# Centroid logits and the feed-forward's product as one weight matrix of 576 columns, in two banks

## The chip, the cores and the metric

The kernel runs on one core of one Trainium2 chip. The metric is the device time of one execution in microseconds (us), taken as the median of several executions. Engines are named as in the profile: PE is TensorE's matmuls and PEld its weight loads, DVE is VectorE, ACT is ScalarE, POOL is GpSimd, and SP is SyncE, which here only issues transfers.

## The reference

One transformer block on `x` of 8 x 256 tokens with 512 features, all in fp32: an attention layer, then a clustered feed-forward layer, each behind a layer norm and with its input added to its output.

```python
def attn(h):                       # 32 heads, 8 key/value heads, D = 128
    q, k, v = split(h @ w_qkv)
    s = q @ k.T * D**-0.5 - slope[head] * sqrt(max(i - j, 0))    # causal
    return (softmax(s) @ v) @ w_o

def ffn(h):                        # h: 2048 x 512
    dots = softmax(h @ centroids.T / 0.1)          # 2048 x 64
    hits = dots > 0.01
    query_sel = any(hits, axis=1)                  # per token
    row_sel = any(hits, axis=0)[assignments]       # per output column
    dense = h @ weight.T + bias                    # 2048 x 512
    return where(query_sel[:, None] & row_sel[None, :], dense, 0)

x = x + attn(layernorm(x))
x = x + ffn(layernorm(x))
```

The feed-forward layer thus has two products with the same left operand, the normalised tokens: 64 columns of logits and 512 columns of output. A column of the output counts only if any token of the whole batch hits its cluster, so that choice can be made only at the very end.

## The kernel before

The 2048 tokens are 16 tiles of 128, and four tiles make a pair of sequences (`p` = 0 to 3). For each pair the kernel goes through the 8 key/value heads, and for each head through the two sequences: 64 units `u`, 16 slots per pair, and two more units to drain. The order of the work on each engine is the order in which the program text issues it (the schedule is manual); buffers come from pools that rotate, and a buffer's next owner waits until its last reader is done. The projections and the output product are done by a seven-product scheme on half blocks (`strassen`, L136, and `project_out`, L454), whose extra sums are made by GpSimd and VectorE.

In unit `u` the kernel computes the scores of unit `u`, subtracts the maximum and takes the exponential of unit `u`-1, and multiplies the weights of unit `u`-2 with the values (`attend`, L429, tiles `av` and `oT`) and with `w_o` (`project_out`, whose banks are `ps_oa`, `ps_ob` and `ps_oc`, and which adds into the residual `x2`). The maxima and sums over keys are made by `over_keys` (L384, tile `r`), transposed by TensorE into `tp_r` (L397), written to a row in memory and read back broadcast to all partitions as `bc` (L406 and L415, both on SP's queue). GpSimd (L422) and VectorE (L425) then subtract the maximum.

The feed-forward layer of a finished tile `t_ffn` is put between these steps as a function `f` of four parts. Tiles 0 to 3 are done in slots 3 to 6 of pair 1, tiles 4 to 7 in the same slots of pair 2, and tiles 8 to 11 in units 62 to 65. Part 0 transposes the normalised tile into `xnT`. Part 1 makes the logits (`ffn_logits`: four matmuls of 64 columns into a bank `lg`, then the negated maximum `cmax` on VectorE, L523 and L524), their exponential on ScalarE (L537), and the dense product (`ffn_dense`: four matmuls of 512 columns into a bank `ps_f`). Part 2 adds the bias (L552), and part 3 finds the hits and finishes the tile. Tiles 12 to 15 (`last` and the next three) are done behind the loop, logits and dense products apart. In the last unit, 65, the next layer norm's statistics (L259 and L260) stand on VectorE directly behind the logits' maximum of tile 11, and the output product adds its parts straight from the banks (L481, L488, L494).

PSUM has eight banks of 512 fp32 columns: three are shared as `acc` (`av`, `ps_f`, `ps_ob`, `ps_oc` and others), two as `sc` (the scores and `lg`), one is `tp` (transposes), and two hold the long sums. The weights of the dense product are loaded into the buffer of the value weights (`wv`) three times: at the end of slot 1 of pairs 1 and 2, and at the end of unit 58. The centroids are loaded once, at the start.

Of the kernel before, what the change touches and what calls it, by code (L numbers as in the profile page):

```python
# [26 lines left out]
NC_H = H // P  # L27
# [6 lines left out]
TEMPERATURE = 0.1  # L34
# [19 lines left out]
def block_kernel(  # L54
# [12 lines left out]
    nc = tc.nc  # L67
# [5 lines left out]
    const = ctx.enter_context(tc.tile_pool(name="const", bufs=1))  # L73
    wpool = ctx.enter_context(tc.tile_pool(name="w", bufs=1))
# [106 lines left out]
    wv, wk, wq, wo = {}, {}, {}, {}  # L181
    HH = H // 2
# [9 lines left out]
        wv[p, half] = [w[:, 2 * k : 2 * k + 2, ts(m, HH)] for m in range(2) for k in range(2)]  # L192

    def load_w_ffn():
        w = wpool.tile([P, NC_H, H], F32, tag="wv", name="w_ffn")
        nc.sync.dma_start(w, w_ffn_t.rearrange("(c p) n -> p c n", p=P))
        return w

    def load_wk(p, j):
# [46 lines left out]
    nc.gpsimd.dma_start(dist_sb, dist)  # L246
    hits_any = const.tile([P, NCL], F32, name="hits_any")
    nc.vector.memset(hits_any, 0.0)
    cent = const.tile([P, NC_H, NCL], F32, name="cent")
    bias_bc = const.tile([P, H], F32, name="bias_bc")  # L250


# [256 lines left out]
    ffn_sb = {}  # L509
    SPLIT = (1, 2, 3)  # L510

    def ffn_logits_product(t):
        xnT = xnT_sb[t]
        lg = p_sc.tile([P, 512], F32, tag="sc", name="lg")
        for c in range(NC_H):
            nc.tensor.matmul(lg[:, :NCL], lhsT=xnT[:, c, :], rhs=cent[:, c, :],
                             start=c == 0, stop=c == NC_H - 1)
        ffn_sb[t] = lg

    def ffn_max(t):  # L520
        lg = ffn_sb[t]
        nmax = small.tile([P, 1], F32, tag="cmax", name="cmax")
        nc.vector.tensor_reduce(nmax, lg[:, :NCL], AX.X, ALU.max, negate=True)  # L523
        nc.vector.tensor_scalar(nmax, nmax, 1.0 / TEMPERATURE, None, ALU.mult)  # L524
        ffn_sb[t] = lg, nmax

    def ffn_logits(t):
        ffn_logits_product(t)
        ffn_max(t)

    def ffn_exp(t, e=None):

        lg, nmax = ffn_sb[t]
        if e is None:
            e = small.tile([P, NCL], F32, tag="e", name="e", bufs=3)
        esum = small.tile([P, 1], F32, tag="esum", name="esum")
        nc.scalar.activation(e, lg[:, :NCL], AF.Exp, bias=nmax, scale=1.0 / TEMPERATURE, accum_out=esum)  # L537
        ffn_sb[t] = e, esum

    def ffn_dense(t, w_ffn, chunks=range(NC_H)):  # L540
        xnT = xnT_sb[t]
        if 0 in chunks:
            y_sb[t] = p_acc.tile([P, 512], F32, tag="acc", name="ps_f")
        ps = y_sb[t]
        for c in chunks:
            nc.tensor.matmul(ps, lhsT=xnT[:, c, :], rhs=w_ffn[:, c, :],  # L546
                             start=c == 0, stop=c == NC_H - 1)

    def ffn_bias_add(t, y=None):
        if y is None:  # L550
            y = work.tile([P, H], F32, tag="y", name="y", bufs=2)
        nc.vector.tensor_add(y, y_sb[t], bias_bc)  # L552
        y_sb[t] = y

    def ffn_hits(t):
# [66 lines left out]
    a_sums(gp, wq[0], "S1 S2")  # L622
    load_wq(1)
    load_wo(0)
    nc.sync.dma_start(cent, centroids_t.rearrange("(c p) n -> p c n", p=P))
    nc.sync.dma_start(bias_bc, ffn_bias.partition_broadcast(P))
    k, q = project_k(0, 0), project_q(0)
    k(1)
# [16 lines left out]
    for u in range(NU + 2):  # L645
# [46 lines left out]
        def f(part):  # L692
            if t_ffn is not None:
                if part == 0:
                    ffn_transpose(t_ffn)
                elif part == 1:
                    ffn_logits(t_ffn)
                    ffn_exp(t_ffn)
                    ffn_dense(t_ffn, w_ffn)
                elif part == 2:  # L700
                    ffn_bias_add(t_ffn, y_late[:, t_ffn % TPP, :] if t_ffn >= first_late else None)
                else:
                    ffn_hits(t_ffn)
                    ffn_qsel(t_ffn)
                    ffn_end(t_ffn)
# [63 lines left out]

        if bb == 0 and own:  # L770
            qq(1), e(1), max_and_old(), e(2), f(0), av(0), e(6), exp_old(), av(1), more_sums(), rows_max(), f(1), e(7), qq(2)
            if u == 4:
                onehot_of_columns(asg)
            f(2), norm(0), e(5), e(4), qq(6), e(3), x(0), w(1), x(1), sum_old(), w(5, 6), norm(1), qq(7), w(2)
            rows(), behind_rows(), w(7, 3), norm(3), w(4)
        elif u < NU - 1:
            e(1), qq(4), e(2), max_and_old(), f(0), e(6), av(0), exp_old(), e(7), av(1), f(1), e(5), qq(5)
            f(2), norm(0), e(4), e(3), x(0), w(1), x(1), sum_old(), w(5, 6), norm(1), qq(3), w(2)
            rows(), behind_rows(), w(7, 3), norm(3), w(4)
        elif own:  # L780

            max_and_old(), f(0), av(0), exp_old(), av(1), rows_max(), f(1)
            f(2), norm(0), w(1), sum_old(), w(5, 6), norm(1), w(2)
            rows(), subtract_max(u, 0), subtract_max(u, 1)
            f(3), norm(2), w(7)
            nc.scalar.activation(s_sb[u], s_sb[u], AF.Exp)
            w(3), norm(3), w(4)
        elif bb == 0:
            sum_old(), av(0), av(1), f(0), rows(), f(1), w(1, 5), f(2), w(6, 2, 7, 3, 4), f(3)
        else:  # L790
            av(0), f(0), av(1), f(1)
            normalise(norm_stats(last, last + 1), tags=("y", "y"))
            ffn_hits(t_ffn), ffn_qsel(t_ffn)
            w(1), f(2), w(2, 5, 6)
            ffn_transpose(last)
            w(3)
            found = norm_root(norm_stats(last + 2))
            ffn_transpose(last + 1, "snap")
            w(7)
            norm_write(norm_scale(found))  # L800
            ffn_logits_product(last), ffn_logits_product(last + 1)
            w(4)


# [52 lines left out]
    ffn_max(last + 1), ffn_exp(last + 1)  # L857
    ffn_transpose(last + 2, copy=nc.vector.tensor_copy)
    ffn_transpose(last + 3, "o_s", tp=p_acc.tile([P, 512], F32, tag="acc", name="tpx_late"), copy=nc.vector.tensor_copy)
    ffn_logits_product(last + 2), ffn_logits_product(last + 3)  # L860
# [32 lines left out]
    for t in range(NT):  # L893
        if t in SPLIT:
            continue
        p, i = divmod(t, TPP)
        if t >= last + 2:
            nc.vector.scalar_tensor_tensor(y_of(i), y_sb[t], ffn_sb[t], y_of(i), ALU.mult, ALU.add)
# [30 lines left out]
```

## Time and profile before

| What | Value |
|---|---|
| Median of 3 runs | 1440.6 us (1440.53 to 1444.04) |
| The profiled execution's time | 1441.13 us |
| Its span, first to last instruction | 1439.4 us |
| Mean granted TensorE clock | 0.996 |
| TensorE matmuls busy | 1407.5 us (98%) |
| VectorE busy | 928.2 us (64%) |
| GpSimd busy | 878.2 us (61%) |
| ScalarE busy | 372.2 us (26%) |
| Memory traffic | 132 GB/s on average |

The page of the profile tells how long each engine was busy, what share each has in the chain of work that ended last, and which groups of instructions cost most. A line of the timeline has the start from the beginning of the span, the time from first start to last end, the engine, the line of the program, the operation, the tiles (out<-in), the shape, and the number of instructions merged in it; in brackets stands the idle time of the engine before it and what ended it. An fp32 matmul appears as two records. Matmuls are pipelined, so a record's duration is longer than its share of the engine's time; the distance from one start to the next is that share. A line of the table of stages has the stage, its length, each engine's busy time with the number of instructions, the granted TensorE clock, the share of the transfer engines in use and GB/s.

### The profile page before, as it was taken

The numbers are of one execution on the slowest core, as the hardware profiler recorded it, in microseconds if no ns is written. First come the engines' busy times: TensorE is split into PE (matmuls) and PEld (weight loads), VectorE is DVE, ScalarE is ACT, GpSimd is POOL, SyncE is SP. The second block draws the span as 40 slices with busy tenths as digits, with TensorE's granted clock in tenths as the row PEclk, the third lists the DMA queues.
The fourth block names the chain that finished last, engine by engine and source line by source line (L and its number), as shares of the span: only waits on it lengthen the run. The fifth ranks groups of instructions, "written<-read, shape, count | busy, mean of one in ns | idle before, by whom it ended". The sixth has DMA issues, their size and how long they took to land.

```text
span 1439.4 us, 16533 instructions
## 1 busy us (share of the span) xinstructions
PE 1407.5 (98%) x5859; PEld 1072.9 (75%) x5859; DVE 928.2 (64%) x1708; ACT 372.2 (26%) x650; POOL 878.2 (61%) x883
## 2 busy tenths in 40 slices
PE   8899999999999999999999999999999999999986
PEld 7677777767877777777777677787777777877663
DVE  5457666686556665667655666566756676556766
ACT  2222223411232222332213312142222211222332
POOL 6377857676464754667555466566747666466543
PEclk9999999999999999999999999999999999999998
DMA  5235433443242544424242425434323353243343
GB/s 190 88 122 176 132 115 136 146 147 132 89 161 74 176 144 150 161 98 142 98 147 102 167 83 176 153 126 147 132 90 117 132 176 132 89 162 103 101 149 117
DMA packets 85968, 189.94 MB, mean 132 GB/s; under 512 B 10592, under 2 KB 18784, under 8 KB 85888
## 3 DMA queue, kind: packets, MB, share of 16 engines
q1 hardware_dynamic: 84736, 186.41, 37.5%
q10 hardware_dynamic: 864, 1.57, 0.3%
q8 instruction: 47, 0.77, 0.2%
q0 software_dynamic: 288, 0.92, 0.2%
q14 instruction: 33, 0.27, 0.1%
HBM read 175.77 MB, written 13.11 MB: 131 GB/s over the span
## 4 chain that ended last, share of the span: by engine, by line
PE 90%; DVE 6%; issue 1%; ACT 1%; POOL 1%; DMA 1%; DVEq 0%; POOLq 0%; ACTq 0%; SPq 0%
PE ps_qa L145 14%; PE ps_oa L468 14%; PE ps_oc L468 7%; PE sc L370 7%; PE ps_qc L145 7%; PE av L446 7%; PE sc L376 4%; PE ps_ob L468 4%; PE ps_ka L145 4%; PE ps_va L145 4%; PE av L447 3%; PE ps_qb L145 3%; PE ps_f L546 3%; PE ps_kc L145 2%; PE ps_vc L145 2%
## 5 line engine op out<-in xcount | busy, mean ns | idle before, releaser
L500 POOL TENSOR_TENSOR x<-x,snap 128x256 f32<-128x256 f32 x189 | 136.0, 736 | 177.5 <-DVE x L488 105.1
L422 POOL TENSOR_TENSOR s<-s,bc 128x1024 f32<-128x1024 f32 x64 | 151.7, 2370 | 150.2 <-DMA bc<-row_hbm 150.0
L387 DVE TRANSPOSE_TENSOR_REDUCE r<-s 128x32 f32<-128x1024 f32 x128 | 158.0, 1234 | 4.5 <-ACT s L735 4.5
L112 POOL TENSOR_TENSOR o_s<-oT 128x256 f32<-128x256 f32 x64 | 47.6, 744 | 180.3 <-DVE oT L450 176.3
L158 ACT COPY qT<-ps_qa 128x512 f32<-128x512 f32 x128 | 74.8, 584 | 289.7 <-PE ps_qa L145 289.6
L483 ACT COPY snap<-ps_oa 128x256 f32<-128x256 f32 x189 | 70.4, 373 | 277.8 <-PE ps_oa L468 277.8
L468 PE MATMUL ps_oa<-wo,oT 128*128 128x256 f32 x512 | 132.7, 381 | 2.6 <-DVE oT L450 2.6
L735 ACT ACTIVATE s<-s 128x1536 f32<-128x1536 f32 x63 | 93.5, 1484 | 148.5 <-DVE s L425 137.8
L446 PE MATMUL av<-s,v 128*128 128x512 f32 x256 | 130.7, 592 | 0.0
L145 PE MATMUL ps_qa<-xT,wq 128*128 128x256 f32 x512 | 121.1, 379 | 0.8 <-ACT qT L158 0.8
L370 PE MATMUL sc<-qT,kT 128*128 128x512 f32 x256 | 120.3, 592 | 0.0
L145 PEld LDWEIGHTS ps_qa<-xT,wq 128*128 128x128 f32 x512 | 97.1, 190 | 27.8 <-issue 16.0
L372 DVE SCALAR_TENSOR_TENSOR s<-sc,alibi 128x512 f32<-128x512 f32 x128 | 88.0, 691 | 30.8 <-PE sc L370 29.8
L468 PEld LDWEIGHTS ps_oa<-wo,oT 128*128 128x128 f32 x512 | 90.9, 190 | 22.6 <-DVE oT L450 5.3
L378 DVE SCALAR_TENSOR_TENSOR s<-sc,alibi 128x512 f32<-128x512 f32 x64 | 44.3, 692 | 85.6 <-PE sc L376 85.6
L447 PEld LDWEIGHTS av<-s,v 128*128 128x128 f32 x256 | 48.6, 190 | 61.2 <-issue 61.2
L450 DVE TENSOR_TENSOR oT<-av,bc 128x512 f32<-128x512 f32 x128 | 83.9, 683 | 11.8 <-PE av L447 10.5
L388 DVE TRANSPOSE_TENSOR_REDUCE r<-s 128x16 f32<-128x512 f32 x128 | 85.6, 669 | 0.0
L447 PE MATMUL av<-s,v 128*128 128x256 f32 x256 | 76.1, 379 | 0.0
L488 DVE TENSOR_TENSOR x<-x,ps_ob 128x256 f32<-128x256 f32 x64 | 26.9, 421 | 73.2 <-PE ps_ob L468 73.1
L370 PEld LDWEIGHTS sc<-qT,kT 128*128 128x128 f32 x256 | 48.6, 190 | 33.9 <-issue 29.9
L494 DVE TENSOR_TENSOR x<-x,ps_oc 128x256 f32<-128x256 f32 x128 | 53.3, 416 | 30.5 <-PE ps_oc L468 29.6
(182 smaller groups left out, 2982.0 us busy)
## 6 DMA issues: line engine op xcount, KB each, us to landing
bc<-row_hbm SPq DMA_DIRECT2D x128, 512.0 KB, 4.8
wq<-in_w_qkv SPq DMA_DIRECT2D x32, 1024.0 KB, 7.7
wo<-in_w_o SPq DMA_DIRECT2D x32, 1024.0 KB, 7.8
alibi<-al_hbm SPq DMA_DIRECT2D x24, 512.0 KB, 8.4
wk<-in_w_qkv SPq DMA_DIRECT2D x16, 512.0 KB, 9.4
wv<-in_w_qkv SPq DMA_DIRECT2D x8, 1024.0 KB, 10.8
x<-in_x SPq DMA_DIRECT2D x16, 256.0 KB, 9.8
al_hbm<-alibi SPq DMA_DIRECT2D x8, 512.0 KB, 9.2
```

The lines of the kernel that those rows point to most:

```text
L145: nc.tensor.matmul(bank[:, cols], lhsT=lhsT, rhs=rhs, start=first and j == 0, stop=j == len(mms) - 1, skip_group_check=True)
L370: nc.tensor.matmul(sc, lhsT=kT[:, t0 : t0 + P], rhs=qT[:, hh : hh + 2, t0 : t0 + S], start=True, stop=True)
L372: nc.vector.scalar_tensor_tensor(s[:, hh * S : (hh + 2) * S], sc, D ** -0.5, bias[:, hh : hh + 2, :].rearrange("p h q -> p (h q)"), ALU.mu ...
L387: nc.vector.tensor_reduce(first, s[:, :K0].rearrange("p (j q) -> p j q", q=32), AX.X, op, apply_transpose=True)
L388: nc.vector.tensor_reduce(second, s[:, K0:].rearrange("p (j q) -> p j q", q=32), AX.X, op, apply_transpose=True)
L422: gp(k0, k0, mx, sub)
L446: nc.tensor.matmul(av, lhsT=v[:, i0, vc], rhs=pT[:, hh * S : (hh + 2) * S], start=True, stop=False)
L447: nc.tensor.matmul(av3[:, :, P:S], lhsT=v[:, i0 + 1, vc], rhs=pT[:, K0 + hh * P : K0 + (hh + 2) * P].rearrange("p (h q) -> p h q", h=2), s ...
L450: ve(oT[:, e].rearrange("p k m q -> p k (m q)"), av3, inv[:, hh : hh + 2, :], ALU.mult)
L468: nc.tensor.matmul(bank[:, :HH], lhsT=x[:, e, :], rhs=y[:, e, :], start=first and e == 0, stop=e == 1, skip_group_check=True)
L500: gp(c, c, s, ALU.add)
L735: nc.scalar.activation(s_sb[u - 1], s_sb[u - 1], AF.Exp)
```

## The change

The centroids become columns 512 to 575 of the tile that holds the dense weights; they come by a second transfer, each time that those weights are loaded. For the twelve tiles that go through `f`, one function makes both products in two banks: a bank of the `sc` pool takes columns 256 to 575 (the second half of the output and the logits, 320 columns), then a bank of the `acc` pool takes columns 0 to 255. The maximum and the exponential are issued behind both. The bias is added in two halves, one for each bank. Tiles 12 to 15 keep their separate products, with the centroids read from the joint tile.

```diff
     def load_w_ffn():
-        w = wpool.tile([P, NC_H, H], F32, tag="wv", name="w_ffn")
-        nc.sync.dma_start(w, w_ffn_t.rearrange("(c p) n -> p c n", p=P))
+        w = wpool.tile([P, NC_H, H + NCL], F32, tag="wv", name="w_ffn")
+        nc.sync.dma_start(w[:, :, :H], w_ffn_t.rearrange("(c p) n -> p c n", p=P))
+        nc.sync.dma_start(w[:, :, H:], centroids_t.rearrange("(c p) n -> p c n", p=P))
         return w
...
-    cent = const.tile([P, NC_H, NCL], F32, name="cent")
...
+    def ffn_product(t, w, at, n, bank, chunks=range(NC_H)):
+        for c in chunks:
+            nc.tensor.matmul(bank[:, :n], lhsT=xnT_sb[t][:, c, :], rhs=w[:, c, at : at + n],
+                             start=c == 0, stop=c == NC_H - 1)
...
+    def ffn_both(t, w_ffn):
+        second = p_sc.tile([P, 512], F32, tag="sc", name="ps_lg")
+        ffn_product(t, w_ffn, HH, HH + NCL, second)
+        first = p_acc.tile([P, 512], F32, tag="acc", name="ps_f")
+        ffn_product(t, w_ffn, 0, HH, first)
+        ffn_sb[t] = second[:, HH : HH + NCL]
+        y_sb[t] = [first[:, :HH], second[:, :HH]]
...
     def ffn_bias_add(t, y=None):
         if y is None:
             y = work.tile([P, H], F32, tag="y", name="y", bufs=2)
-        nc.vector.tensor_add(y, y_sb[t], bias_bc)
+        n = H // len(y_sb[t])
+        for h, ps in enumerate(y_sb[t]):
+            nc.vector.tensor_add(y[:, ts(h, n)], ps, bias_bc[:, ts(h, n)])
         y_sb[t] = y
...
-    nc.sync.dma_start(cent, centroids_t.rearrange("(c p) n -> p c n", p=P))
     nc.sync.dma_start(bias_bc, ffn_bias.partition_broadcast(P))
...
                 elif part == 1:
-                    ffn_logits(t_ffn)
+                    ffn_both(t_ffn, w_ffn)
+                    ffn_max(t_ffn)
                     ffn_exp(t_ffn)
-                    ffn_dense(t_ffn, w_ffn)
```

More of the change, by code (lines that the diff above doesn't have):

```diff
@@ L510, in block_kernel, with ffn_logits_product, ffn_dense @@
     SPLIT = (1, 2, 3)
-    def ffn_logits_product(t):
-        xnT = xnT_sb[t]
-        lg = p_sc.tile([P, 512], F32, tag="sc", name="lg")
[L515 to L518, printed above, removed]
+    def ffn_product(t, w, at, n, bank, chunks=range(NC_H)):
+        for c in chunks:
+            nc.tensor.matmul(bank[:, :n], lhsT=xnT_sb[t][:, c, :], rhs=w[:, c, at : at + n],
+                             start=c == 0, stop=c == NC_H - 1)
+    def ffn_logits_product(t, w_ffn):
+        lg = p_sc.tile([P, 512], F32, tag="sc", name="lg")
+        ffn_product(t, w_ffn, H, NCL, lg)
+        ffn_sb[t] = lg[:, :NCL]
+    def ffn_dense(t, w_ffn, chunks=range(NC_H)):
+        if 0 in chunks:
+            y_sb[t] = [p_acc.tile([P, 512], F32, tag="acc", name="ps_f")]
+        ffn_product(t, w_ffn, 0, H, y_sb[t][0], chunks)
+    def ffn_both(t, w_ffn):
[5 more added lines that the diff above has]
+        y_sb[t] = [first[:, :HH], second[:, :HH]]
     def ffn_max(t):
@@ L522, in ffn_max @@
         nmax = small.tile([P, 1], F32, tag="cmax", name="cmax")
-        nc.vector.tensor_reduce(nmax, lg[:, :NCL], AX.X, ALU.max, negate=True)
+        nc.vector.tensor_reduce(nmax, lg, AX.X, ALU.max, negate=True)
         nc.vector.tensor_scalar(nmax, nmax, 1.0 / TEMPERATURE, None, ALU.mult)
         ffn_sb[t] = lg, nmax
-    def ffn_logits(t):
-        ffn_logits_product(t)
-        ffn_max(t)
     def ffn_exp(t, e=None):
@@ L536, in ffn_exp @@
         esum = small.tile([P, 1], F32, tag="esum", name="esum")
-        nc.scalar.activation(e, lg[:, :NCL], AF.Exp, bias=nmax, scale=1.0 / TEMPERATURE, accum_out=esum)
+        nc.scalar.activation(e, lg, AF.Exp, bias=nmax, scale=1.0 / TEMPERATURE, accum_out=esum)
         ffn_sb[t] = e, esum
[L540 to L547, printed above, removed]
     def ffn_bias_add(t, y=None):
@@ L800, in block_kernel @@
             norm_write(norm_scale(found))
-            ffn_logits_product(last), ffn_logits_product(last + 1)
+            ffn_logits_product(last, w_ffn), ffn_logits_product(last + 1, w_ffn)
             w(4)
@@ L859, in block_kernel @@
     ffn_transpose(last + 3, "o_s", tp=p_acc.tile([P, 512], F32, tag="acc", name="tpx_late"), copy=nc.vector.tensor_copy)
-    ffn_logits_product(last + 2), ffn_logits_product(last + 3)
+    ffn_logits_product(last + 2, w_ffn), ffn_logits_product(last + 3, w_ffn)
     ffn_max(last + 2), ffn_exp(last + 2)
@@ L897, in block_kernel @@
         if t >= last + 2:
-            nc.vector.scalar_tensor_tensor(y_of(i), y_sb[t], ffn_sb[t], y_of(i), ALU.mult, ALU.add)
+            nc.vector.scalar_tensor_tensor(y_of(i), y_sb[t][0], ffn_sb[t], y_of(i), ALU.mult, ALU.add)
         if p < NPAIR - 2:
```

## The prediction

> **What bounds the kernel now.** I read the page's busy times and its chain first, then the timeline around one feed-forward tile, then the last 110 us. The page:
>
> ```profile
> PE 1407.5 (98%) x5859; PEld 1072.9 (75%) x5859; DVE 928.2 (64%) x1708; ACT 372.2 (26%) x650; POOL 878.2 (61%) x883
> ...
> PE 90%; DVE 6%; issue 1%; ACT 1%; POOL 1%; DMA 1%; DVEq 0%; POOLq 0%; ACTq 0%; SPq 0%
> ```
>
> TensorE is busy 98% of the span and is 90% of the chain that ended last, so a change to its passes is felt nearly everywhere. It runs an fp32 product as two records per matmul ("passes" below): four chunks give eight. TensorE's timeline at the first tile:
>
> ```profile
> 426.00 1.02 PE L446 MATMUL av<-s,v 128*128 128x512 f32 x2
> 426.86 0.59 PE L447 MATMUL av<-s,v 128*128 128x256 f32 x2
> 427.29 1.00 PE L516 MATMUL lg<-cent,xnT_xnT 128*128 128x64 f32 x8
> 428.12 3.65 PE L546 MATMUL ps_f<-w_ffn,xnT_xnT 128*128 128x512 f32 x8
> 431.61 1.03 PE L145 MATMUL ps_kc<-xT_t,e_t 128*128 128x256 f32 x4
> ```
>
> Durations overlap here; what counts is start to start. Two 512-column passes take 426.86 - 426.00 = 0.86, so 0.429 us each; two of 256 take 0.43, so 0.216. The difference, 0.213 us for 256 columns, is 0.833 ns a column with about 2.6 ns fixed. The whole tile takes 431.61 - 427.29 = 4.32 us (4.327 unrounded). Eight passes of 512 are 3.434 of it; the 64-column ones have 0.893, or 0.112 each, though by the line through the other two sizes they would need 0.056. The weight loads do not fit underneath them; under 256 columns they do.
>
> **The change part by part.**
>
> *Passes of the twelve loop tiles.* Removed: 8 x 0.112 + 8 x 0.429 = 4.327. Added: 8 passes of 320 columns and 8 of 256. No row has 320; it lies between the measured 256 and 512, and the line gives 320 x 0.833 + 2.6 = 269 ns. Bounds: 0.216 (as 256) and 0.429 (as 512); I take 0.269, nearest to the 256 row. Sum 8 x 0.269 + 8 x 0.216 = 3.882, a saving of 0.445 us a tile. Columns and weight loads stay the same in number; the saving is the uncovered weight load. The last four tiles keep separate products: no change.
>
> *The eight middle tiles* (slots 3 to 6 of pairs 1 and 2). The table of stages shows TensorE busy for the whole 4.3 or 4.4 us of each, and its passes follow without a gap from 400 to 520 and from 776 to 870 us. The nearest outside condition is the transpose tp_r behind the sums r: the smallest margin in these units is 0.81 us (third tile of each pair), and I use up 0.445 and at most 0.15 of it. So 8 x 0.445 = 3.56 us come through.
>
> *The longer wait of cmax.* The logits used to be ready 1.00 us after the product began; now after seven pitches of 0.269, a first step of 0.056 and a last pass of some 0.43: 2.37. VectorE's in-order queue stands 1.37 us longer at cmax, and the exponential on ScalarE is later by as much. What is queued behind it:
>
> ```profile
> 428.58 0.15 DVE L524 TENSOR_SCALAR cmax<-cmax 128x1 f32<-128x1 f32 x1
> ...
> 432.75 0.42 DVE L165 TENSOR_TENSOR kT<-kT,ps_kc 128x256 f32<-128x256 f32 x1 [4.01 <-PE ps_kc L145]
> ```
>
> VectorE idles 3.5 to 4.0 us there in all eight middle tiles, 2.5 in the first two tail tiles, 5.9 in the third, because the next operation needs a product that TensorE makes after the tile. After the saving at least 2.0 is left, so 1.37 is free in eleven tiles; if that cover were gone it would cost 1.37 a tile. ScalarE has 1.95 us or more behind the exponential in the same tiles. The twelfth has no such cover.
>
> *Bias add in two halves.* 2 x 0.416 (row L494) against 0.684 (L552): 0.15 us of VectorE by durations; start to start 2 x 0.33 against 0.61, 0.05. Hidden by the same idle time in the middle; counted in the tail below. The bank ps_lg is held until the second half is done, but its pool's next claim on it is the second score product of the next unit, over 10 us later.
>
> *Loads.* One centroid load leaves the start, where no engine waits for it; nothing gained. Three are added behind w_ffn on SP's queue:
>
> ```profile
> w_ffn<-in_w_ffn_t SPq DMA_DIRECT2D x3, 1024.0 KB, 9.8
> ...
> cent<-in_centroids_t SPq DMA_DIRECT2D x1, 128.0 KB, 9.8
> ```
>
> The issue took SP 0.89 us at 12.5. At 400.7 SP then has nothing until 415.3, at 750.8 until 764.7, and after 1283.7 it is free likewise. By the row the data are there some 11 us after the issue, against 26 or more to first use. [...] without cover, some 10 us.
>
> *Tail, first and second tile* (1345.6 and 1362.0). The first pays 0.445: TensorE runs without a gap from it to the second. The second doesn't:
>
> ```profile
> 1366.50 0.69 DVE L552 TENSOR_TENSOR y_late<-ps_f,bias_bc 128x512 f32<-128x512 f32 x1 [2.51 <-PE ps_f L546]
> ...
> 1368.80 2.35 POOL L422 TENSOR_TENSOR s<-s,bc 128x1024 f32<-128x1024 f32 x1 [2.28 <-DMA bc<-row_hbm]
> ...
> 1370.56 0.63 DVE L390 TENSOR_TENSOR r<-r 128x16 f32<-128x16 f32 x1
> ...
> 1371.33 0.27 PE L397 MATMUL tp_r<-ident,r 128*64 128x128 f32 x1 [1.41 <-DVE r L390]
> ```
>
> TensorE waits for L390, a tiny operation that takes 0.63 instead of 0.18 and ends at 1371.19, as GpSimd's L422 ends (1371.15). L422 waits for a transfer whose row was made before the second tile's product. So everything up to the third tile comes 0.445 earlier, not 0.89.
>
> *Third tile* (1379.9): TensorE-bound onward, 0.445. *Fourth* (1394.9), VectorE's and then TensorE's rows:
>
> ```profile
> 1395.98 0.23 DVE L523 TENSOR_REDUCE cmax<-lg 128x1 f32<-128x64 f32 x1
> ...
> 1400.34 0.42 DVE L481 TENSOR_TENSOR x<-x,ps_oa 128x256 f32<-128x256 f32 x1 [0.70 <-PE ps_oa L468]
> 1400.67 0.68 DVE L552 TENSOR_TENSOR y_late<-ps_f,bias_bc 128x512 f32<-128x512 f32 x1
> 1401.28 0.41 DVE L488 TENSOR_TENSOR x<-x,ps_ob 128x256 f32<-128x256 f32 x1
> 1402.06 0.42 DVE L494 TENSOR_TENSOR x<-x,ps_oc 128x256 f32<-128x256 f32 x1 [0.38 <-PE ps_oc L468]
> ```
>
> ```profile
> 1402.72 0.60 PE L290 MATMUL tpx<-ident,xn 128*128 128x128 f32 x4
> 1403.16 1.03 PE L468 MATMUL ps_oc<-wo,o_s 128*128 128x256 f32 x4
> ```
>
> Behind cmax stand the statistics of the next norm, whose xn the transpose at 1402.72 needs, and the reads of ps_oa and ps_oc, before which TensorE may not add to those banks again. The product starts 0.89 earlier, at 1394.05; cmax then at 1396.42 instead of 1395.98, 0.5 us late. The chain of statistics moves to xn done near 1400.2, against a transpose now wanted at 1401.4: covered. L481 comes near 1400.1, the halves to 1400.7, L488 1401.1, L494 1401.4 to 1401.85; TensorE wants ps_oc at 1401.83. A stall of some 0.05: 0.4 of 0.445 is paid. By durations instead of starts (L494 ends near 1402.3) the stall is 0.45 and this tile pays nothing.
>
> *Clock.* The stage from 1379.7 to 1384.2 ran at a granted clock of 0.62 on average:
>
> ```profile
> 1379.70:1384.20 4.50, 4.43 (x14) 2.79 (x15) 2.13 (x6) 0.41 (x2) 4.01 (x5) 0.62 1.05 393
> ```
>
> That is half rate for about 3.4 us, a loss of 1.7, after TensorE had stood idle 1.2 and 1.4 us from 1376 to 1380. By the row it stays: those two gaps hang on the same chain and keep their length, and 1435.8 stands. [...]
>
> *Sum.* 3.56 + 0.445 + 0 + 0.445 + 0.4 = 4.85 us. Profiled execution: 1441.1, of which 1439.4 span and 1.7 around it; span after 1434.6, time 1436.3. The median shown, 1440.6, is 0.5 below that execution, so on its footing **1435.8**.
>
> **The rivals.**
> - *All twelve tiles pay*: 12 x 0.445 = 5.3, 1435.3. For it: 90% of the chain is TensorE; against it, L422's transfer wait in the tail.
> - *A wait takes the place of the work*: the fourth tail tile loses its 0.4 and more to VectorE's late queue, or some middle margin (0.81) is used up, or another half-clock stretch: 1436.2 to 1437.5.
> - *The half-clock stretch falls away*: 1434.1.
> - *Slower: the 320-column pass is dear.* Place: the added passes of ps_lg. At 0.325 us a pass the tile breaks even ((4.327 - 1.728)/8); at the upper bound 0.429 a tile takes 5.16, 0.83 more, and twelve give 1440.6 + 10 = 1450.6. For it: no row has that size; against it: 256 and 512 lie on a line with hardly a fixed part.
>
> That the change doesn't merge the products is excluded: the changed program's order of instructions has 320 and 256 columns at all twelve places.
>
> **How the numbers follow.** Main case 0.55 (its own range 1435.3 to 1436.3), all twelve 0.08, wait or extra stretch 0.23, stretch gone 0.09, dear pass 0.05. A measurement of this kernel can tell about 0.3%, 4.3 us: faster means under 1436.3. The main case nearly whole, all twelve and the stretch gone give 0.67, some of the main case's edge taken off: 0.65. Slower: 0.05. Same: 0.30. Range: 1434.0 to 1437.6, leaving out the dear pass and the worst of the waits.
>
> **What would show it.** Start to start of ps_lg's passes 0.269 and of ps_f's 0.216, 3.88 us from a tile's first pass to the next work in twelve places; cmax near 2.4 us after it with VectorE's idle time behind it still over 1.5; L422 in the second tail unit ending level with L390; the fourth tail tile's L494 level with the ps_oc product. Wrong if ps_lg's passes are over 0.3 us, if a tp_r in slots 3 to 6 begins to wait for r, or if the half-clock stretches differ in number.

## The result, and the profile after

| What | Before | After |
|---|---|---|
| Median time, run side by side (22 runs each) | 1440.8 us | 1437.7 us |
| Ratio of the times, with its 95% interval | | 0.9975 (0.9967 to 0.9982) |
| The profiled execution's time | 1441.1 us | 1438.6 us |
| Its span | 1439.4 us | 1436.8 us |
| TensorE matmuls busy | 1407.5 us | 1404.8 us |

The change saves 3.6 us by the ratio (2.6 to 4.8), where 4.85 was forecast. That is a gain beyond doubt, but at the edge of the 0.3% (4.3 us) that was named as what a measurement can tell. The same program measured again among the experiments gave 0.9968 (0.9960 to 0.9975).

The page after, its busy times:

```profile
PE 1404.8 (98%) x5859; PEld 1082.3 (75%) x5859; DVE 928.7 (65%) x1720; ACT 372.4 (26%) x650; POOL 877.6 (61%) x883
...
DVE 1%; PE 1%; issue 0%; ACT 0%; DVEq 0%; ACTq 0%
```

TensorE has as many matmuls as before and is 2.7 us less busy; VectorE has twelve operations more, one more half of the bias in each of twelve tiles. The chain of waits (second line) can be followed back over only some 2% of this span, so unlike before it says nothing of the bound, and I go by the timeline.

The first tile, in the timeline after. A line has the start, the time to the last end, the engine, the line of the program, the tiles, and in brackets the idle time before it:

```profile
427.44 0.59 PE L448 MATMUL av<-s,v 128*128 128x256 f32 x2
...
427.87 2.32 PE L515 MATMUL ps_lg<-w_ffn,xnT_xnT 128*128 128x320 f32 x8
...
430.02 1.89 PE L515 MATMUL ps_f<-w_ffn,xnT_xnT 128*128 128x256 f32 x8
...
430.22 0.23 DVE L540 TENSOR_REDUCE cmax<-ps_lg 128x1 f32<-128x64 f32 x1 [1.46 <-PE ps_lg L515]
...
431.75 1.03 PE L145 MATMUL ps_kc<-xT_t,e_t 128*128 128x256 f32 x4
...
432.88 0.42 DVE L165 TENSOR_TENSOR kT<-kT,ps_kc 128x256 f32<-128x256 f32 x1 [2.25 <-PE ps_kc L145]
```

From start to start, the eight passes of 320 columns take 430.02 - 427.87 = 2.15 us (0.269 each), and the eight of 256 take 431.75 - 430.02 = 1.73 (0.216). The tile takes 3.88 instead of 4.32 (4.33 unrounded) in eleven of the twelve places. In the first tail tile it takes 3.95:

```profile
1344.18 0.27 PE L398 MATMUL tp_r<-ident,r 128*32 128x128 f32 x1 [1.25 <-DVE r L391]
1344.31 2.39 PE L515 MATMUL ps_lg<-w_ffn,xnT_xnT 128*128 128x320 f32 x8
1346.53 1.89 PE L515 MATMUL ps_f<-w_ffn,xnT_xnT 128*128 128x256 f32 x8
1348.26 1.03 PE L469 MATMUL ps_oa<-wo,oT 128*128 128x256 f32 x4
```

The eight wide passes have 2.22 us there instead of 2.15; the first of them alone has 0.344. In the first tile `cmax` starts 2.35 us after the product begins, and VectorE still idles 2.25 us before L165, where it idled 4.01.

How far this reaches the end is seen from one `tp_r` to a later one, in us. The first six rows have separate products in the tail's four tiles, the last six joint ones. The two last columns also hold half-clock stretches (3.41 us at a granted TensorE clock of 0.50, as from 1380.19 us before and from 1370.75 after), which fall elsewhere from profile to profile:

| Kernel (experiments named below) | Four middle tiles, either pair | First tail tile's unit | Second tail tile's unit | Third tail tile to the end |
|---|---|---|---|---|
| before | 94.52 | 16.38 | 17.91 | 59.59 |
| before again | 94.52 | 16.38 | 17.99 | 58.78 |
| widths undone | 94.52 | 16.38 | 18.03 | 59.43 |
| loads alone | 94.52 | 16.38 | 18.02 | 59.46 |
| loads thrice | 94.52 | 16.38 | 17.56 | 59.60 |
| middle only | 92.73 | 16.38 | 17.93 | 59.47 |
| after | 92.73 | 16.02 | 18.03 | 58.58 |
| after again | 92.73 | 16.02 | 17.85 | 59.04 |
| loads back later | 92.73 | 16.02 | 17.92 | 58.82 |
| 448 and 128 | 92.81 | 16.04 | 17.80 | 57.99 |
| 448, back later | 92.81 | 16.04 | 17.67 | 58.72 |
| quarters | 92.73 | 16.02 | 18.03 | 58.79 |

The four tiles of a pair give 1.79 us, 0.447 a tile, in every profile with the split at 256 (1.71 with 448 and 128). The first tail tile gives 0.36, as its first pass is longer and the step from the transpose to it takes 0.125 us instead of 0.108. The second gives nothing (17.91 and 17.88 on average). For the rest the means of six rows and six differ by 0.73, which would make 3.58 + 0.36 + 0 + 0.73 = 4.67 in all, but these rows differ in where the stretch lies, and two have other loads. Like beside like is better:

- With a stretch in the third tail tile, the five profiles with separate tail products have 59.43 to 59.60, and quarters, the one with joint products and the loads in place, has 58.79: a gain of 0.72. The third tile has 0.44 of it (15.06 us from the third tile's product to the fourth's, then 14.62), the fourth the rest.
- With a stretch near 1417 us instead, before again has 58.78 and after again 59.04. The third tile gains 0.46 here too (13.40, then 12.94), and behind the fourth tile's product 0.71 is lost (45.28, then 45.99). This is one profile against one.

So the sum is 4.66 in the one case and 3.68 in the other. Two kernels are left out of the table: one with another order of the products, and one with a double half-clock stretch in the third tail tile (61.06 us in the last column).

The two spans first compared differ by only 2.6. Most of the remainder was lost where the change touches nothing: 1.21 us in the units from 245 to 327 us, where a half-clock stretch fell at 302.4 (these units have 81.93 us after and 80.72 before, but 81.86 in before again, which has such a stretch at the same place), and 1.23 in the unit from 1210 to 1236 us (25.49, where before has 24.26), in which a transfer came late:

```profile
1213.56 0.79 SPq L416 DMA_DIRECT2D bc<-row_hbm  x2
...
1219.61 2.35 POOL L423 TENSOR_TENSOR s<-s,bc 128x1024 f32<-128x1024 f32 x1 [2.07 <-DMA bc<-row_hbm]
...
1220.57 1.43 DVE L391 TENSOR_TENSOR r<-r 128x16 f32<-128x16 f32 x1
...
1223.35 0.89 PE L145 MATMUL ps_va<-wv,xT 128*128 128x256 f32 x3 [0.98 <-DVE wv L116]
```

The broadcast took 6.0 us from issue to landing (4.0 at this place before), GpSimd's subtraction came late and overlapped VectorE's L391, and TensorE waited. After again has 24.26 in this unit like before, and loads alone (below), without the joint product, has 25.59, so that it isn't the change's doing.

The second tail tile after, the place where the prediction let nothing through:

```profile
1364.39 0.42 DVE L558 TENSOR_TENSOR y_late<-ps_f,bias_bc 128x256 f32<-128x256 f32 x1 [1.31 <-PE ps_f L515]
1364.74 0.41 DVE L558 TENSOR_TENSOR y_late<-ps_lg,bias_bc 128x256 f32<-128x256 f32 x1
...
1367.29 2.34 POOL L423 TENSOR_TENSOR s<-s,bc 128x1024 f32<-128x1024 f32 x1 [2.41 <-DMA bc<-row_hbm]
...
1368.52 1.14 DVE L391 TENSOR_TENSOR r<-r 128x16 f32<-128x16 f32 x1
...
1369.81 0.27 PE L398 MATMUL tp_r<-ident,r 128*64 128x128 f32 x1 [2.00 <-DVE r L391]
```

TensorE's wait grew from 1.41 to 2.00 us, more than the tile saved. L391 ends at 1369.66, as GpSimd's L423 does (1369.63): it stands 1.14 us for what takes 0.17 at its shortest.

The fourth tail tile after, with SP's queue from 1374 us on:

```profile
1374.10 0.44 SPq L852 DMA_DIRECT2D back_xT<-x_hbm  x1
1374.58 0.51 SPq L852 DMA_DIRECT2D back_xT<-y_hbm  x1
1375.13 0.76 SPq L852 DMA_DIRECT2D back_wq<-x_hbm  x1
1375.93 1.12 SPq L852 DMA_DIRECT2D back_wq<-y_hbm  x1
1380.29 0.32 SPq L407 DMA_DIRECT2D row_hbm<-row  x1
1389.74 0.33 SPq L416 DMA_DIRECT2D bc<-row_hbm  x1
```

```profile
1391.29 2.32 PE L515 MATMUL ps_lg<-w_ffn,xnT_xnT 128*128 128x320 f32 x8
...
1393.67 1.29 DVE L451 TENSOR_TENSOR oT<-av,bc 128x512 f32<-128x512 f32 x2 [2.86 <-PE ps_lg L515]
1394.88 0.21 DVE L540 TENSOR_REDUCE cmax<-ps_lg 128x1 f32<-128x64 f32 x1
...
1398.68 0.41 DVE L482 TENSOR_TENSOR x<-x,ps_oa 128x256 f32<-128x256 f32 x1
...
1399.24 1.10 PE L469 MATMUL ps_oa<-wo_t,o_s 128*128 128x256 f32 x4 [1.32 <-DVE x L482]
```

The row of unit 64 (L407), issued at 1380.29, landed 9.4 us later, with four loads for the last stage issued ahead of it on the same queue; the other 66 rows of this profile land in 1.3 to 3.6 us. Its broadcast, issued at 1389.74, landed at 1393.55 and released L451. The bracket names `ps_lg` as what ended that wait, but L451 doesn't read it. VectorE stands 2.86 us there, everything behind it is late, and TensorE waits 1.32 us for L482. Before, the row took 9.1 us as well, but VectorE was at work until 1394.46 on its own, and the broadcast landed at 1394.43, level with it; before again, without a stretch in the third tile, has the wait. Their lines, before first:

```profile
1393.71 0.75 DVE L572 SCALAR_TENSOR_TENSOR y_late<-y_late,qsel,x 128x512 f32<-128x512 f32 x1
1394.55 1.29 DVE L450 TENSOR_TENSOR oT<-av,bc 128x512 f32<-128x512 f32 x2
```

```profile
1391.78 0.75 DVE L572 SCALAR_TENSOR_TENSOR y_late<-y_late,qsel,x 128x512 f32<-128x512 f32 x1
1394.45 1.29 DVE L450 TENSOR_TENSOR oT<-av,bc 128x512 f32<-128x512 f32 x2 [1.92 <-DMA bc<-row_hbm]
```

The table of stages, of the stretch with the halved clock after (stage, length, busy times and counts, granted clock, transfer share, GB/s):

```profile
1369.50:1375.00 5.50, 5.19 (x15) 4.06 (x16) 5.23 (x14) 2.54 (x3) 3.75 (x4) 0.69 0.08 14
```

Before it lay in the third tail tile (from 1380.2), after it lies behind the second (from 1370.7).

### The profile page after: what moved, and what is told of

Same layout as the page of the kernel before. It is cut to its first block, busy times and chain, and to the rows that moved or that the text cites. A ratio compares the mean times of both kernels' runs of the same rounds, so it can differ in the third digit from the quotient of the medians.

```text
span 1436.8 us, 16560 instructions
## 1 busy us (share of the span) xinstructions
PE 1404.8 (98%) x5859; PEld 1082.3 (75%) x5859; DVE 928.7 (65%) x1720; ACT 372.4 (26%) x650; POOL 877.6 (61%) x883
## 5 line engine op out<-in xcount | busy, mean ns | idle before, releaser
L423 POOL TENSOR_TENSOR s<-s,bc 128x1024 f32<-128x1024 f32 x64 | 151.7, 2371 | 151.4 <-DMA bc<-row_hbm 151.3
L388 DVE TRANSPOSE_TENSOR_REDUCE r<-s 128x32 f32<-128x1024 f32 x128 | 158.0, 1234 | 4.3 <-ACT s L740 4.3
L451 DVE TENSOR_TENSOR oT<-av,bc 128x512 f32<-128x512 f32 x128 | 83.9, 682 | 15.1 <-PE av L448 10.5
L389 DVE TRANSPOSE_TENSOR_REDUCE r<-s 128x16 f32<-128x512 f32 x128 | 85.6, 669 | 0.0
L391 DVE TENSOR_TENSOR r<-r 128x16 f32<-128x16 f32 x128 | 69.6, 543 | 4.4
```

What stands on the lines that cost most here:

```text
L388: nc.vector.tensor_reduce(first, s[:, :K0].rearrange("p (j q) -> p j q", q=32), AX.X, op, apply_transpose=True)
L389: nc.vector.tensor_reduce(second, s[:, K0:].rearrange("p (j q) -> p j q", q=32), AX.X, op, apply_transpose=True)
L423: gp(k0, k0, mx, sub)
L451: ve(oT[:, e].rearrange("p k m q -> p k (m q)"), av3, inv[:, hh : hh + 2, :], ALU.mult)
```

## The experiments

*My theory*: the gain is the weight load of the 64-column passes, hidden under wider ones, in eleven of the twelve tiles; the loads and the later `cmax` cost nothing. *Rivals*: something else of the change pays or costs (its loads, the bias in halves, the order), and the late `cmax` or the late row takes gain away in the last tail tile. Each experiment has its ratio to the kernel before, run side by side on the same chip.

**Widths undone** (the changed kernel with 64 and 512 columns again):

```diff
-        ffn_product(t, w_ffn, HH, HH + NCL, second)
+        ffn_product(t, w_ffn, H, NCL, second)
...
-        ffn_product(t, w_ffn, 0, HH, first)
-        ffn_sb[t] = second[:, HH : HH + NCL]
-        y_sb[t] = [first[:, :HH], second[:, :HH]]
+        ffn_product(t, w_ffn, 0, H, first)
+        ffn_sb[t] = second[:, :NCL]
+        y_sb[t] = [first[:, :HH], first[:, HH:]]
```

> Everything of the change but the widths: 64 and 512 columns again, in the same two kinds of bank, with the joint weight tile, three centroid loads and the bias added in two halves. Weight-load theory (the saving is the time by which a weight load exceeds a 64-column pass): a loop tile takes 4.33 us again, the eight middle tiles give nothing, and the time is that of the kernel before within 1 us (ratio 0.9995 to 1.0007). Rival (part of the gain comes from the loads or from the start, where the centroids no longer come): the ratio stays at 0.999 or less with tiles of 4.33 us.

Measured: 1.0007 (0.9999 to 1.0015), 1442.7 us. The first tile in its timeline:

```profile
426.98 1.00 PE L515 MATMUL ps_lg<-w_ffn,xnT_xnT 128*128 128x64 f32 x8
427.82 3.65 PE L515 MATMUL ps_f<-w_ffn,xnT_xnT 128*128 128x512 f32 x8
431.31 1.03 PE L145 MATMUL ps_kc<-xT_t,e_t 128*128 128x256 f32 x4
```

4.33 us again, and the whole gain is gone. What is left of the change (three loads, the joint tile, bias in halves, the maximum behind both products) gains nothing. The widths are the whole effect. That the floor of the narrow passes is the weight load is read from the loads' own records, in the kernel before:

```profile
427.07 1.08 PEld L516 LDWEIGHTS lg<-cent,xnT_xnT 128*128 128x128 f32 x8
428.07 0.30 PEld L546 LDWEIGHTS ps_f<-w_ffn,xnT_xnT 128*128 128x128 f32 x2
428.61 0.19 PEld L546 LDWEIGHTS ps_f<-w_ffn,xnT_xnT 128*128 128x128 f32 x1 [0.24 <-issue]
```

From the second on, the loads for the narrow passes start 0.112 us apart with no idle time between them, which is the passes' own distance; between those for the 512-column passes 0.24 us are idle.

**Middle only** (the tail's four tiles unmerged):

```diff
-                    ffn_both(t_ffn, w_ffn)
-                    ffn_max(t_ffn)
-                    ffn_exp(t_ffn)
+                    if t_ffn < first_late:
+                        ffn_both(t_ffn, w_ffn)
+                        ffn_max(t_ffn)
+                        ffn_exp(t_ffn)
+                    else:
+                        ffn_logits_product(t_ffn, w_ffn)
+                        ffn_max(t_ffn)
+                        ffn_exp(t_ffn)
+                        ffn_dense(t_ffn, w_ffn)
```

> The joint products in the eight middle tiles alone; the four tail tiles make their logits and dense products apart as before, from the joint weight tile. Transfer theory: of the tail's four tiles only the first pays, so this loses 0.4 us against the changed kernel: 3.2 to 3.6 us faster than before, ratio 0.9975 to 0.9978. TensorE theory (eleven tiles pay): it loses 1.3 us against the changed kernel and the changed kernel should then stand at 0.9966.

Measured: 0.9974 (0.9963 to 0.9984). The eight middle tiles pay in full (forecast 3.56 us, a ratio of 0.9975). The tail's 1.1 is too small to be told from this by whole times; the table above has it.

**Loads alone** and **loads thrice** (the kernel before, with the centroids loaded each time, once and three times over, to find a price by its growth):

```diff
         nc.sync.dma_start(w, w_ffn_t.rearrange("(c p) n -> p c n", p=P))
+        nc.sync.dma_start(cent, centroids_t.rearrange("(c p) n -> p c n", p=P))
...
-    nc.sync.dma_start(cent, centroids_t.rearrange("(c p) n -> p c n", p=P))
```

> The kernel before with the centroid load moved alone: none at the start, one behind each of the three loads of the dense weights, into the same separate tile. Forecast of the loads' price: nothing, ratio 0.9995 to 1.0005. Rival (the series with everything but the widths, at 1.0007, hints at it): the three added transfers cost 0.5 to 1.5 us, ratio 1.0005 to 1.0010, and a broadcast behind one of them lands over 1 us later than in the kernel before.

> The kernel before with no centroid load at the start and three of them (the same data into the same separate tile) behind each load of the dense weights, nine in all. If the 1.0011 of the loads alone is a price of the loads, this pays it three times for the last two thirds: ratio 1.002 to 1.004. If it was chance, the ratio is 0.9995 to 1.0010, like that of one load, and the units in which the loads land are as long as in the kernel before.

Measured: 1.0011 (1.0003 to 1.0020) with three loads, which looked like a price of 1.6 us and missed what was expected; 1.0009 (1.0000 to 1.0018) with nine. A price per load would have tripled. The units in which the loads are issued keep their length in every profile (87.5 to 87.6 us around 400, 18.22 around 750, 76.0 to 76.3 around 1283), and the half-clock stretches in the first kernel's profile, at 62 and 1387 us, lie 340 us before the first load and 100 behind the last. The loads have no price that shows. In all profiles an added load that is issued directly behind the dense weights lands 9.4 to 13.0 us after its issue, when those weights land too (9.4 to 11.8 without it); in loads thrice, the second and third of each place, which come when the weights have landed, take 2.1 to 2.3. An arrangement with one load and a copy into the joint tile wasn't tried.

**Before again** and **after again** (the two kernels unchanged, to see how far a ratio wanders):

> The kernel before, unaltered, measured like any other kernel against itself: what a difference in these series is worth. Ratio 0.9993 to 1.0007, and a profile whose tiles take 4.33 us, with half-clock stretches and waits for broadcasts at other places than in its first profile. If the ratio is 1.0010 or 0.9990, the 1.0011 of the loads alone and the 0.9968 to 0.9975 of the changed kernel are no more exact than that.

> The changed kernel itself, unaltered, once more, for a second profile and more times beside the other kernels of this series. Reading so far: eight middle tiles pay 0.445 us each in every profile, the tail 1.2; what is left of the difference comes from half-clock stretches and broadcast landings that fall differently in each execution. Then this profile has 3.88 us for each of the twelve tiles again, other places of waiting outside them than the first one had, and the ratio is 0.9966 to 0.9980. If instead the waits from 870 to 1320 us sit at the same places as in the first profile, they belong to the change.

Measured: 1.0005 (0.9997 to 1.0013), and 0.9968 (0.9960 to 0.9975). Five kernels without the joint widths (before again, widths undone, loads alone, loads thrice, and the kernel before with its loads back later, below) average 1.0006; seven with them in the given order average 0.9973. The difference of 0.0033, or 4.8 us, is the forecast's size. It is an average over kernels that differ in other things as well (one has the joint widths in eight tiles only), so it supports the 4.85 and doesn't prove it.

**Loads back later** (the four loads of the last stage one unit later, so that the row of unit 64 isn't behind them), on the changed kernel and on the one before:

```diff
-        if u == NU - 1:
+        if u == NU:
```

> The changed kernel with its four loads of 1 MB that bring tiles 0 to 7 back issued one unit later, behind unit 64's row transfer instead of ahead of it. Transfer theory (the third and fourth tail tiles pay nothing, as unit 64's row lands behind 4 MB and VectorE's oT of unit 65 waits for its broadcast): the row lands in under 3 us instead of 9, VectorE doesn't idle before that oT, the wait of 1.3 us before ps_oa in unit 65 goes, and the time falls by 1 to 2 us below the changed kernel: ratio to the kernel before 0.9960 to 0.9970. TensorE theory (the tail was bound by TensorE anyway, or by VectorE's late cmax): no change against the changed kernel, ratio 0.9975.

> The kernel before with the four 1 MB loads issued one unit later. Transfer theory: without a half-clock stretch in the tail, the row wait bounds it before the change too, but with less to win, since TensorE comes later by two to three tiles' 0.445 us: 0 to 1 us faster, ratio 0.9993 to 1.0000. If the transfer is no bound here at all: 1.0000 with the span's end unchanged. Together with e2 this gives the change's worth with the tail free: by the transfer theory 10 to 11 tiles of 0.445, 4.4 to 4.9 us.

Measured: 0.9969 (0.9958 to 0.9981) on the changed kernel, 0.9997 (0.9989 to 1.0005) on the one before. The fourth tail tile of the first, in the timeline:

```profile
1393.69 1.46 DVE L451 TENSOR_TENSOR oT<-av,bc 128x512 f32<-128x512 f32 x2
...
1394.26 2.32 PE L515 MATMUL ps_lg<-w_ffn,xnT_xnT 128*128 128x320 f32 x8
...
1396.62 0.23 DVE L540 TENSOR_REDUCE cmax<-ps_lg 128x1 f32<-128x64 f32 x1 [1.46 <-PE ps_lg L515]
```

The row now lands 1.35 us after its issue, and L451 waits for nothing: that the four loads held the row up is shown. With it gone, `cmax` is what VectorE stands at, 2.36 us after the tile began, as the prediction drew it, and TensorE meets no wait before L482's bank in that unit. But the time isn't measurably better than the changed kernel's (0.9968 for after again), where 1 to 2 us were expected. In this profile a half-clock stretch lay in the third tile, with which the row's wait is small anyway; that the same holds for the other executions isn't shown. Between the two kernels with late loads the change is worth 0.0028, or 4.0 us (4.4 to 4.9 expected).

**448 and 128** (the logits with 64 of the output's columns, so that they are ready 1.26 us sooner), and the same with the loads back later:

```diff
+    NF = 448
...
-        ffn_product(t, w_ffn, HH, HH + NCL, second)
+        ffn_product(t, w_ffn, NF, H + NCL - NF, second)
...
-        ffn_product(t, w_ffn, 0, HH, first)
+        ffn_product(t, w_ffn, 0, NF, first)
```

> The joint product split at column 448: 128 columns (64 of output, 64 of logits) in the first bank, then 448 in the other; the bias added in 448 and 64 columns. Line with a floor (start to start is the larger of 0.112 us, the weight load, and 0.833 ns a column + 2.6 ns): passes of 0.112 and 0.376 us, a tile of 3.90 us, and the time within 0.5 us of the changed kernel. The logits are ready some 1.1 us after the tile's first pass instead of 2.4, so cmax is as early as before the change. If a wide pass had its own price (steps at 256 or 512 columns), the tile would be 4.2 us or more.

> The split at column 448 together with the four 1 MB loads issued behind unit 64's row: early logits and an early broadcast. If these are what holds the tail, VectorE doesn't idle for the broadcast before unit 65's oT nor at cmax for over 0.3 us, no wait over 0.3 us stands before ps_oa, and in executions without a half-clock stretch in unit 64 the tail is 1 to 1.5 us shorter than the changed kernel's: ratio 0.9958 to 0.9970. If the tail's end is set by something later (norm of the last tile, the copies of the output), the wait goes and the time stays at the changed kernel's.

Measured: 0.9975 (0.9964 to 0.9986) and 0.9975 (0.9963 to 0.9986). The first tile of the first:

```profile
427.81 1.05 PE L516 MATMUL ps_lg<-w_ffn,xnT_xnT 128*128 128x128 f32 x8
428.70 3.17 PE L516 MATMUL ps_f<-w_ffn,xnT_xnT 128*128 128x448 f32 x8
431.71 1.03 PE L145 MATMUL ps_kc<-xT_t,e_t 128*128 128x256 f32 x4
```

0.89 and 3.01 us: 0.112 for 128 columns, as for 64 (the line has 0.109), and 0.376 for 448, on the line. The line and the floor thus hold at six widths, 64 to 512. In the tail L451 still stood 2.23 us for the broadcast: earlier logits don't help where the row is late. With both edits neither wait is there, and the time is no better, where 0.9958 to 0.9970 was expected: the runs can't tell this version from the changed kernel.

**Swapped** (the 256-column product first, so that `cmax` comes 1.73 us later still):

```diff
-        second = p_sc.tile([P, 512], F32, tag="sc", name="ps_lg")
-        ffn_product(t, w_ffn, HH, HH + NCL, second)
         first = p_acc.tile([P, 512], F32, tag="acc", name="ps_f")
         ffn_product(t, w_ffn, 0, HH, first)
+        second = p_sc.tile([P, 512], F32, tag="sc", name="ps_lg")
+        ffn_product(t, w_ffn, HH, HH + NCL, second)
```

> The changed kernel with the two banks' products in the other order: 256 columns first, then the 320 with the logits. The tile stays at 3.88 us, but the logits are ready 4.0 us after its first pass instead of 2.4, so VectorE stands longer at cmax. Cover theory: in the middle 0.5 us or more of VectorE's idle time is still left behind cmax, so the middle costs nothing; in the last loop unit the whole chain behind cmax (norm statistics, reads of ps_oa) comes some 1.3 to 1.6 us later, and the product that waits for the read of ps_oa with it: 1 to 1.6 us slower than the changed kernel, with the wait before ps_oa in unit 65 at 1.4 us or more. If cmax's lateness costs in the middle too, it is 4 us or more slower.

Measured: 0.9986 (0.9976 to 0.9997), 0.0018 or 2.6 us above after again, which ran beside it. The middle's four tiles keep their 92.73 us with `cmax` at its latest: the idle time that was named as cover is cover. The price is in the tail, where the fourth tile reads:

```profile
1391.15 1.29 DVE L451 TENSOR_TENSOR oT<-av,bc 128x512 f32<-128x512 f32 x2 [2.19 <-DMA bc<-row_hbm]
1391.16 2.32 PE L515 MATMUL ps_lg<-w_ffn,xnT_xnT 128*128 128x320 f32 x8
...
1393.51 0.23 DVE L540 TENSOR_REDUCE cmax<-ps_lg 128x1 f32<-128x64 f32 x1 [1.08 <-PE ps_lg L515]
...
1397.66 1.10 PE L469 MATMUL ps_oa<-wo_t,o_s 128*128 128x256 f32 x4 [1.59 <-DVE x L482]
```

Both waits one after the other. From the first tail tile on its profile is 0.78 us longer than after again's (0.22 in the first tile's unit, 0.05, 0.51); the rest of the 2.6 isn't located. The two intervals together leave 1.9 us either way, so some price is certain, and the rest beyond 0.78 can just be chance.

**Quarters** (the changed kernel with GpSimd's subtraction in the second tail tile's unit as four instructions):

```diff
-            gp(k0, k0, mx, sub)
+            step = 1 if u == NU - 1 else G
+            for h in range(0, G, step):
+                gp(k0[:, h : h + step], k0[:, h : h + step], mx[:, h : h + step], sub)
```

> The changed kernel with GpSimd's subtraction of the maximum (128 x 1024) cut into four operations of 256 columns for unit 63 alone. Theory: VectorE's tiny L391 in the second tail unit isn't slow by itself but stands until GpSimd's operation in progress ends; then it takes 0.7 us or less instead of 1.1, and the transpose behind it starts 0.4 us or more earlier against GpSimd's start. Rival: VectorE gets no turn before GpSimd's whole run of operations is over, or L391 is late for its own data: it takes as long as before.

Measured: 0.9973 (0.9963 to 0.9982).

```profile
1366.72 2.79 POOL L425 TENSOR_TENSOR s<-s,bc 128x256 f32<-128x256 f32 x4 [2.30 <-DMA bc<-row_hbm]
...
1368.07 0.17 DVE L391 TENSOR_TENSOR r<-r 128x16 f32<-128x16 f32 x1
...
1368.39 0.27 PE L398 MATMUL tp_r<-ident,r 128*64 128x128 f32 x1 [1.03 <-DVE r L391]
```

L391 takes 0.17 instead of 1.14 us and TensorE's wait falls from 2.00 to 1.03: L391 does stand until the instruction that GpSimd is in has ended, and short ones let it through sooner. The profile after has 32 cases in which L391 starts inside an L423, and in all of them it ends 0.03 to 0.15 us behind that L423, after 0.18 to 2.06 us. The reductions just ahead of it (L388, L389) aren't held up: 43 and 33 of them start inside an L423 there, and take 1.23 and 0.67 us like the others (1.24 and 0.67). Why the one kind stands and the other doesn't is not shown. The gain is given back within the next unit, where the next `tp_r` waits 1.85 us: the four pieces together are longer (2.79 us against 2.34), and VectorE's scaling of `e` (L566) took 1.07 us where it took 0.53.

## Why the prediction was right, and where not

- *Passes of the twelve tiles*: right to the third digit in eleven. 320 columns were put at 0.269 and measured 0.269; the tile 3.882 and 3.880. This takes away the rival of the dear pass. The first tail tile has 3.955.
- *The eight middle tiles*: 3.56 forecast, 3.58 found in every profile.
- *The longer wait of `cmax`*: 2.37 us after the product's start forecast, 2.35 found (the sum's first step of 0.056 isn't in the trace, too little to matter); free in the middle, which the swapped order shows with a harder case.
- *Bias in halves* (0.41 us each): hidden, as widths undone shows, where it remains and costs nothing measurable. *Loads*: nothing, by nine of them as by three. The three added loads landed 10.0 to 10.7 us after their issue, near the 11 read from the row.
- *Tail, first tile*: 0.445 forecast, 0.36 found. *Second*: nothing, for the reason given, and the reason is shown by quarters.
- *Third tile*: 0.445 forecast, 0.44 and 0.46 found.
- *Fourth tile*: this is the step that failed. The prediction set this tile's end by the lateness of `cmax` alone, and paid 0.4. It left out that the row of unit 64 stands behind four loads on SP's queue. In the profile before this couldn't be seen as a wait, because the half-clock stretch in the third tile held TensorE and VectorE up until just the moment at which the broadcast landed (1394.46 and 1394.43): a wait of nothing with no margin. With the stretch elsewhere, VectorE stands 1.9 us for the broadcast in the kernel before and 2.2 to 2.9 in those with joint products. With the stretch in the third tile the forecast for both tiles, 0.845, came near (0.72); with the stretch elsewhere the fourth tile gave back what the third had gained, in the one pair of profiles that can be compared.
- *Clock: "By the row it stays"*: it didn't; the stretch moves between profiles of the same program (1380 and 1419 us in two of the kernel before). Taking one profile's stretch as fixed was wrong, and not only for the stretch's own 1.7 us (15.06 against 13.40 for the third tile in two profiles of the kernel before): the fourth tile's gain hangs on it. That a stretch could come or go was not shown by the profile before; the 1437.5 and 1434.1 were my estimate, from the 1.7 us that this one cost.
- *The sum*: 4.85 forecast, 3.7 to 4.7 by the stages, 3.6 (2.6 to 4.8) and 4.6 (3.6 to 5.8) by the two measurements. The time of 1435.8 stood on a median of 1440.6, from which the first ratio makes 1437.0, inside the range; the first median itself was 1437.7, just over its end of 1437.6, the second 1437.6 against a before of 1442.0. That the mean came so near is in part luck, since the fourth tile's share depends on a stretch that moves. What failed here is the range's ground: it counted only cases of the change, and the kernel's own wandering by a stretch (1.2 to 1.7 us) or a late broadcast (1.2 us) belongs in it. For the same reason 0.65 for faster by over 0.3% was too much for a gain of 4.85 with a bound of 4.3.

What stays open: why the first pass of the first tail tile takes 0.344 us, how often the stretch falls in the third tail tile, and which part of the swapped order's 2.6 us isn't chance.

## What to carry to other kernels

Fit the time of a pass against its columns from rows of the trace; where narrow passes lie on a floor above that line (here 0.112 us against 0.056 at 64 columns), their columns are free to be joined with others, and the gain is the floor's excess times the number of passes, however the joint width is cut. Before counting a saving near the end of a program, look at margins of zero: an arrival that is level with the work it releases becomes the bound as soon as the work comes earlier. And a forecast of 0.3% on a kernel whose own runs wander by that much needs a range that says so.

## What the runs showed of the hardware

- *Half-clock stretches.* In those of before and after the granted clock is 0.50. Each lasts 3.413 us (once 6.827), but for the last of each profile, which reaches to its end; and all distances between the stretches of a profile are whole multiples of 3.413 us: 17, 74, 313 and 403 of them among those found (313 and 17 in the profile after). In two profiles of the kernel before the stretches fall at different places (1380 and 1431 us; 302, 1419 and 1432 us). The 3.41 us just ahead of the stretches of before (1380.2) and after (1370.8), and 3.41 us of before with no stretch behind them (stage, length, busy times and counts from PE on, clock, transfers):

```profile
1376.78:1380.19 3.41, 1.16 (x10) 0.87 (x9) 3.35 (x7) 2.35 (x4) 3.15 (x4) 1.00 0.87 311
```

```profile
1367.33:1370.75 3.42, 1.43 (x8) 0.96 (x7) 3.32 (x7) 1.60 (x3) 3.42 (x2) 1.00 0.01 2
```

```profile
1366.54:1369.95 3.41, 3.38 (x16) 2.57 (x14) 3.34 (x7) 1.22 (x3) 1.15 (x1) 1.00 0.34 123
```

TensorE is busy for 1.16 and 1.43 us of 3.41 ahead of these stretches, 34% and 42%, and for 3.38 in the third line. Counting in steps of 3.413 us from the stretches, from 30 us on and leaving out the last stretch of each profile, it is busy for 34% ahead of the one stretch of before and for 59% or more in the 407 other steps, and for 52% and 42% ahead of the two of after and 65% or more in the 404 others. In all fourteen profiles the 21 steps just ahead of a stretch have 22 to 58%; of the 5,683 others at full clock none has under 45%, and fifteen lie between 45 and 58%. So the two overlap, and what brings a stretch is not shown. That the stretches' places are what makes one execution differ from the next by 1 to 5 us is my estimate from these profiles, not shown.
- *fp32 passes.* 0.833 ns a column and 2.6 ns, at 256, 320, 448 and 512 columns; 0.112 us at 64, and at 128, where this line has 0.109.
- *A small transfer behind large ones.* A row that took 9.4 us with four loads issued ahead of it on the same queue landed in 1.35 us when it was issued ahead of them.
- *VectorE and GpSimd.* A VectorE operation of 16 columns (L391, profile after) took 1.14 and 1.43 us instead of 0.17 while GpSimd was in an instruction of 2.34 and 2.35 us, and ended 0.03 us behind it.
